# Moving work between the stages of a two-layer Mamba, attention and expert kernel: gates, decay loads, gathering, and the product delta u

## The chip, the cores and the metric

The kernel runs on one core of a Trainium2 chip. The metric is the device time in microseconds (us) of one execution; a time stated for a kernel is the median of its runs. Five engines of the core work beside each other, each on its own queue of instructions, in order: TensorE (PE) for matrix products, VectorE (DVE), ScalarE (ACT), GpSimd (POOL) and SyncE (SP). SP issues most of the loads, POOL most of the stores, and ACT some loads. Everything is float32.

## The reference

Four images of 64 x 64 tokens with 128 channels go through two layers.

```python
# layer 0: three selective scans over the 4096 tokens of an image
xz = in_proj_w @ group_norm(x)              # 256 rows for x, 256 for z
def mamba_dir(xz):                          # forward, backward, and sliced order
    x, z = split(xz)
    x = silu(causal_conv1d(x))              # called u in the kernel
    dt, B, C = split(x_proj_w @ x)          # 8, 16 and 16 rows
    delta = softplus(dt_w @ dt + dt_b)
    h = 0                                   # 256 x 16 states
    for t in tokens:
        h = h * exp(delta[t] * A) + (delta[t] * x[t]) * B[t]     # A = -exp(A_log)
        y[t] = sum_n(h * C[t])
    return (y + D * x) * silu(z)
x = x + out_proj_w @ (mamba_f + mamba_b + mamba_s)

# layer 1, attention: 16 heads of 8 channels, q = k = v
q = ring(cos(layer_norm(x) + theta))
ctx = softmax(q q^T / sqrt(8)) q            # then projection, norm, a small FFN, norm

# layer 1, experts: each of 64 experts chooses its 8 best tokens of an image
probs = softmax(gate_w @ layer_norm(t), over tokens)
topv, topi = top_k(probs, 8)
pooled[e] = sum_k topv[k, e] * layer_norm(t)[topi[k, e]]
answer[e] = [gelu([pooled[e], 1] @ weight1[e]), 1] @ weight2[e]
t[topi] += topv * answer
```

## The kernel before

The order of the work is written out by hand. Pieces of work are Python generators that yield between groups of instructions; a `Pace` hands out so many of those yields for each round of something else, and `flow(pieces, width, apart)` interleaves up to `width` pieces, the next one beginning once the one before has come `apart` yields far. The order in which instructions are handed out is the order in which each engine gets them.

**Loading.** `scan_weights` loads and transposes weights for the three scans. At its end it loads `A_log` of each direction with 32 small DMAs (0.5 KB each), half on the ACT queue and half on the POOL queue, 96 in all.

**The fill.** `Inputs.pieces` makes what the scans of all four images need. For each image it normalises x (`norm`), and then, for each of three orders and four chunks of 1024 tokens (`of_chunk`), makes u, B, C and delta and stores them in DRAM. delta is a softplus put together from ACT, PE and DVE steps (lines 400 to 427). Line 431 then multiplies delta by u, in place in the tile `u`, and stores the product `du`. `gate` computes silu(z) of one quarter of the image; its tile comes from the same pair of buffers as `u`. The four gates of an image follow the four chunks of the third order. Beside this work, `Scans.of_image(0, ...)` already scans image 0, with 1.5 yields of inputs for each yield of the scan.

**A scan.** `of_image` has 384 steps for an image: 12 chunks, each of 8 x 4 steps. A tile of 128 rows holds 16 channels with 8 states each, so two steps share a load. `load` broadcasts delta and du from DRAM (512 KB each) two steps ahead, mostly on SP. `exp` is ACT's exponential of delta A; `inputs` multiplies du by B on DVE; `step` runs the scan instruction on DVE, has POOL copy its last column into `ends`, and multiplies by C; `total` sums over states on PE, and `out` adds D u and stores. The tiles of delta have three buffers, those of du four.

**The loops.** `Attention.opening(b)` combines the scans of image b into the attention's input. `Attention.loop(b, beside)` has 1024 rounds, each with scores (`s`), softmax exponentials (`e`, two ACT instructions) and values (`acc`). Beside the loops of images 0 to 2 run the scans of the next images, and what follows or precedes an image (`after`, `opening`). These are the scanning loops. Beside the loop of image 3, called the last loop, `last` runs at 0.8 yields a round: the rest of image 2, the experts' search and choice for images 0 to 2, and image 3 block by block as far as its attention is done. `block.bank` is a single PSUM bank there.

**The tail.** After the last loop, `closing` finishes the eighth block of image 3, and `gathers` is handed out between its steps, at 3.0 yields for each. It is `experts.gather(range(nb - 1))`, 24 pieces of `pool`. Each piece loads a block of 512 normalised tokens, turns the chosen weights into columns with PE (`wt`, line 1198), copies them (`wT`, line 1204) and multiplies (`pool`, line 1209). Then come choice and gathering for image 3, the experts' weights, streamed through few rooms, and the answers scattered to the output.

Of the kernel before, what the change touches and what calls it, by code (L numbers as in the profile page):

```python
# [11 lines left out]
F32 = mybir.dt.float32  # L12
# [4 lines left out]
P = 128  # L17
# [7 lines left out]
T = 1024  # L25
# [109 lines left out]
def scan_weights(nc, const, load, load_ps, ident, in_proj_w, out_proj_w, dirs):  # L135

    w_z = const["fill"].tile([P, DI], F32, name="w_z")
    w_out = const["all"].tile([P, 2, C], F32, name="w_out")
    w_in = load.tile([P, 4, C], F32, tag="w_in", name="raw_in")
    nc.sync.dma_start(out=w_in, in_=in_proj_w.rearrange("(k p) c -> p k c", p=P))  # L140
    ps = load_ps.tile([P, 512], F32, tag="ps", name="ps_in")
    for m in range(2):
        nc.tensor.transpose(ps[:, m * P : (m + 1) * P], w_in[:, 2 + m, :], ident)
    nc.vector.tensor_copy(w_z, ps[:, :DI])
    raw = load.tile([P, DI], F32, tag="raw", name="raw_out")
    nc.sync.dma_start(out=raw, in_=out_proj_w)
    ps = load_ps.tile([P, 512], F32, tag="ps", name="ps_out")
    for m in range(2):
        nc.tensor.transpose(ps[:, m * P : (m + 1) * P], raw[:, m * P : (m + 1) * P], ident)
    nc.vector.tensor_copy(w_out.rearrange("p m c -> p (m c)"), ps[:, :DI])  # L150
    ws = []
    for i, d in enumerate(dirs):
        w = {}
        raw = load.tile([R + 2 * NS, DI], F32, tag="raw", name=f"raw_x{i}")
        nc.sync.dma_start(out=raw, in_=d["x_proj_w"])
        w["x"] = const["fill"].tile([P, 2, X_ROWS], F32, name=f"w_x{i}")
        nc.gpsimd.memset(w["x"], 0.0)
        for m in range(2):
            ps = load_ps.tile([P, 512], F32, tag="ps", name=f"ps_x{i}_{m}")
            k = R + 2 * NS  # L160
            nc.tensor.transpose(ps[:, :k], raw[:, m * P : (m + 1) * P], ident[:k, :k])
            for row, at, n in [(32 * g, 0, R) for g in range(4)] + [(B_ROW, R, NS), (C_ROW, R + NS, NS)]:
                nc.vector.tensor_copy(w["x"][:, m, row : row + n], ps[:, at : at + n])
        raw = load.tile([P, 2, X_ROWS], F32, tag="raw_dt", name=f"raw_dt{i}")
        nc.gpsimd.memset(raw, 0.0)
        for g in range(4):
            by = (nc.sync, nc.scalar)[g % 2]
            by.dma_start(out=raw[:, :, 32 * g : 32 * g + R], in_=d["dt_proj_w"].rearrange("(m p) r -> p m r", p=P))
        w["dt"] = const["fill"].tile([X_ROWS, 2, P], F32, name=f"w_dt{i}")
        ps = load_ps.tile([P, 512], F32, tag="ps", name=f"ps_dt{i}")  # L170
        for m in range(2):
            nc.tensor.transpose(ps[:X_ROWS, m * P : (m + 1) * P], raw[:, m, :], ident)
        nc.vector.tensor_copy(w["dt"].rearrange("r m p -> r (m p)"), ps[:X_ROWS, :DI])
        for name in ("conv_b", "dt_proj_b"):
            w[name] = const["fill"].tile([P, 2], F32, name=f"{name}{i}")
            nc.scalar.dma_start(out=w[name], in_=d[name].rearrange("(m p) -> p m", p=P))

        w["D"] = const["all"].tile([P, DI // 32], F32, name=f"D{i}")
        for g in range(4):
            nc.scalar.dma_start(out=w["D"][32 * g : 32 * g + 32], in_=d["D"].rearrange("(k p) -> p k", p=32))  # L180

        taps = load.tile([P, 2, 4], F32, tag="taps", name=f"taps{i}")
        nc.scalar.dma_start(out=taps, in_=d["conv_w"].rearrange("(m p) k -> p m k", p=P))
        w["conv"] = const["fill"].tile([P, 4, DI], F32, name=f"conv{i}")
        for k in range(4):
            ps = load_ps.tile([P, 512], F32, tag="ps", name=f"ps_cv{i}_{k}")
            for m in range(2):
                cut = load.tile([P, C], F32, tag="cut", name=f"cut{i}_{k}_{m}")
                nc.vector.tensor_scalar_mul(cut, w_in[:, m, :], taps[:, m, k : k + 1])
                nc.tensor.transpose(ps[:, m * P : (m + 1) * P], cut, ident)  # L190
            nc.vector.tensor_copy(w["conv"][:, k, :], ps[:, :DI])
        ws.append(w)
    for i, (d, w) in enumerate(zip(dirs, ws)):

        w["A"] = const["all"].tile([P, 2, NB // 2], F32, name=f"A{i}")
        a_log = d["A_log"].rearrange("(k d) (q n) -> d q n k", d=16, n=NS2)
        for c in range(16):
            for q, by in enumerate((nc.scalar, nc.gpsimd)):
                by.dma_start(out=w["A"][c * NS2 : (c + 1) * NS2, q, :], in_=a_log[c, q])
    return w_z, w_out, ws  # L200


class Inputs:
# [38 lines left out]
    def pieces(self, images):  # L242

        for b in images:
            self.sz[b] = self.dram.tile([DI, L], F32, name=f"d_sz_{b}")
            yield self.norm(b)
            for order in range(3):
                if order == 2:
                    yield self.slices(b)
                for c in range(NC):  # L250
                    yield self.of_chunk(b, order, c)
                    if order == 2:
                        yield self.gate(b, c)

    def norm(self, b):

# [77 lines left out]
    def of_chunk(self, b, order, c):  # L334
# [93 lines left out]
            self.leave()  # L428
        self.middle = False
        keep("delta", r)  # L430
        nc.vector.tensor_mul(u, r, u)
        keep("du", u)
        self.made[b, order, c] = made
        yield

# [1 line left out]
class Scans:  # L437
# [23 lines left out]
    def of_image(self, b, made, alone=False):  # L461
# [54 lines left out]
        def step(s):  # L516

            order, c, k, j = steps[s]
            at = 4 * k + j
            dA, dB = tiles.pop(("delta", s)), tiles["du", s]  # L520
            h = self.deep.tile([P, T], F32, tag="h", bufs=2, name=f"h_{b}_{s}")
            first = 0.0 if c == 0 else ends[order, c - 1][:, at : at + 1]
            nc.vector.tensor_tensor_scan(h, dA, dB, first, ALU.mult, ALU.add)  # L523
            if c < NC - 1:
                nc.gpsimd.tensor_copy(ends[order, c][:, at : at + 1], h[:, T - 1 :])  # L525
            if s + 1 < n:
                inputs(s + 1)
            nc.vector.tensor_mul(dB, h, spread[order, c, "C", j % 2])  # L528

        def total(s, y):  # L530
            order, c, k, j = steps[s]
# [836 lines left out]
def tile_kernel(tc, ctx, x, in_proj_w, dirs, out_proj_w, attn, gate, weight1, weight2, out):  # L1368
# [15 lines left out]
    with ExitStack() as fill:  # L1384
        consts = {"all": all_const, "fill": fill.enter_context(tc.tile_pool(name="w_fill", bufs=1))}
        with tc.tile_pool(name="w_load", bufs=2) as load, tc.tile_pool(
            name="w_load_ps", bufs=2, space=PSUM
        ) as load_ps:
            w_z, w_out, made = scan_weights(nc, consts, load, load_ps, ident, in_proj_w, out_proj_w, dirs)
        ws.extend(made)  # L1390
        inputs = Inputs(tc, fill, x, w_z, ws, cols, dram, ident)
        scans.bank = Bank(fill.enter_context(tc.tile_pool(name="s_bank", bufs=2, space=PSUM)), 2)
        with tc.manual_schedule():
            first = Pace(scans.of_image(0, inputs.made, True))
            others = Pace(flow(inputs.pieces(range(nb)), 2, 10))
            while not first.done:
                others.run(1.5)
                first.run(1.0)
            others.rest()
# [12 lines left out]
    block.bank = bank  # L1412
    loop = ExitStack()
    block.begin(loop)
    with tc.manual_schedule():
        last = Pace()
        n = 3 * NC * NB
# [32 lines left out]
    with tc.manual_schedule():  # L1450
        last = Pace(
            last.parts, experts.biases(),
            *(part for images in pairs[:-1] for part in (experts.search(images, blocks), experts.choice(images, blocks))),
            block.after(nb - 1, range(0, 4)), block.after(nb - 1, range(4, 6)), block.after(nb - 1, range(6, blocks - 1)),
            experts.search(pairs[-1], blocks - 1),
        )
        block.loop(nb - 1, lambda i: last.run(0.8), True)
        last.rest()
    loop.close()
    with ExitStack() as end:  # L1460
        block.bank = Bank(end.enter_context(tc.tile_pool(name="end_ps", bufs=7, space=PSUM)), 7)
        with tc.manual_schedule():
            room = experts.room(end, 3)
            gathers = Pace(experts.gather(range(nb - 1)))
            with ExitStack() as pieces:
                block.pieces_of(pieces, 1, opening=False)
                closing = block.after(nb - 1, range(blocks - 1, blocks), experts.rest(pairs[-1], blocks - 1))
                for i, _ in enumerate(closing):
                    if i == 2:
                        experts.prefetch(room, nc.scalar)  # L1470
                    gathers.run(3.0)
            for _ in experts.choice(pairs[-1], blocks - 1):
                gathers.run(3.0)
            gathers.rest()
            experts.prefetch(experts.room(end, 1), nc.scalar)
            for _ in experts.gather(pairs[-1]):
                pass
            for _ in experts.answers(end, out):
# [33 lines left out]
```

## Time and profile before

| What | Value |
|---|---|
| Time, median of 3 runs | 12982.96 us (12969.35 to 12983.24) |
| Profiled execution, its own time | 12992.53 us |
| Its span | 12990.6 us |
| PE busy | 12191.8 us, 94% of the span |
| ACT busy | 10713.3 us, 82% |
| DVE busy | 8718.2 us, 67% |
| POOL busy | 2930.0 us, 23% |
| DMA moved | 1481.86 MB, 114 GB/s on average |
| SP's DMA queue | 1055.63 MB, 31.8% of 16 engines' span |

The profile is of one execution. The stages follow each other: loading to about 58 us, the fill to 2273 us, the opening of image 0 to 2598, the loops of images 0 to 2 to about 10240, the last loop to 12680, then the tail. In a row of the profile, `out<-in` names the tiles, `x` the number of instructions, then come busy time in us and the mean in ns of one, and then the idle time of the engine just ahead of them with what ended it. A busy share of PE is a modelled one, and the average over the span mixes stages that different engines limit; so shares are read by stage.

### The profile page before, as it was taken

What the parts mean: (1) busy time and instruction counts of PE and PEld (TensorE: products, weight loads), DVE (VectorE), ACT (ScalarE), POOL (GpSimd) and SP (SyncE); (2) the same over time, 40 slices, a digit from 0 to 9 for tenths busy, and PEclk for the clock granted to TensorE, in tenths of its full rate; (3) what the DMA queues carried; (4) which work ended last, traced back from release to release, by engine and by line L of the source; (5) the groups of instructions that cost most, each with busy time, mean ns of one, the idle gap of its engine ahead of it and who ended that gap; (6) DMA issues with size and microseconds to landing.
All of it is one profiled execution on the core that took longest, in us unless ns stands there. A gap on an engine that the chain in (4) does not pass through costs nothing.

```text
span 12990.6 us, 213981 instructions
## 1 busy us (share of the span) xinstructions
PE 12191.8 (94%) x85447; PEld 3937.0 (30%) x85447; DVE 8718.2 (67%) x8674; ACT 10713.3 (82%) x10808; POOL 2930.0 (23%) x3817
## 2 busy tenths in 40 slices
PE   7788888399999999999999999999999999999996
PEld 3333333122222222333322223333222223322225
DVE  6999999788888777888887778888874211121112
ACT  5676766399999988999999889999998888888881
POOL 3323232221212212223232123232321000000000
PEclk9898988699999999999999999999999999999996
DMA  5666776555444455444444445444443100000005
GB/s 157 195 202 195 208 199 190 159 124 122 119 122 111 111 132 134 125 117 111 115 110 110 130 132 126 117 110 116 112 110 97 51 19 11 18 24 11 16 14 183
DMA packets 688512, 1481.86 MB, mean 114 GB/s; under 512 B 187694, under 2 KB 304998, under 8 KB 687254
## 3 DMA queue, kind: packets, MB, share of 16 engines
q1 hardware_dynamic: 499294, 1055.63, 31.8%
q0 software_dynamic: 140192, 302.80, 7.6%
q10 hardware_dynamic: 48024, 109.74, 3.3%
q8 instruction: 669, 10.96, 0.4%
q14 instruction: 333, 2.73, 0.1%
HBM read 1158.77 MB, written 308.81 MB: 113 GB/s over the span
## 4 chain that ended last, share of the span: by engine, by line
PE 81%; DVE 7%; ACT 5%; issue 4%; DMA 3%; SPq 0%; POOL 0%; ACTq 0%; DVEq 0%; POOLq 0%
PE s L881 36%; PE acc L895 30%; PE y L534 4%; PE cv L364 3%; DVE h L523 3%; PE sp L422 2%; PE fo L1033 1%; ACT e L886 1%; PE h L1023 1%; PE xd L378 1%; DVE dB L514 1%; ACT ln L415 0%; DVE du L514 0%; PE out L761 0%; DVE r L427 0%
## 5 line engine op out<-in xcount | busy, mean ns | idle before, releaser
L886 ACT ACTIVATE e<-s 128x1024 f32<-128x1024 f32 x8192 | 7904.8, 1027 | 1053.5 <-PE s L881 882.8
L881 PE MATMUL s<-qm,qT 32*128 32x512 f32 x32768 | 5444.3, 642 | 120.8 <-ACT e L886 61.5
L895 PE MATMUL acc<-e,v 128*32 128x512 f32 x32768 | 4387.5, 607 | 23.8 <-ACT av L904 21.3
L881 PEld LDWEIGHTS s<-qm,qT 32*128 32x128 f32 x32768 | 1801.7, 184 | 3239.3 <-issue 1429.4
L525 POOL COPY ends<-h 128x1 f32<-128x1 f32 x1152 | 1275.0, 1108 | 3352.1 <-DVE h L523 3322.4
L895 PEld LDWEIGHTS acc<-e,v 128*32 128x32 f32 x32768 | 649.0, 108 | 3160.9 <-issue 3021.8
L523 DVE TENSOR_TENSOR_SCAN h<-delta,ends,du 128x1024 f32<-128x1024 f32 x576 | 1350.9, 2345 | 216.2 <-ACT delta L507 185.5
L523 DVE TENSOR_TENSOR_SCAN h<-dA,ends,dB 128x1024 f32<-128x1024 f32 x576 | 1350.6, 2345 | 149.2 <-ACT dA L507 145.8
L514 DVE TENSOR_TENSOR dB<-du,B 128x1024 f32<-128x1024 f32 x768 | 927.9, 1208 | 626.8 <-PE y L534 603.6
L507 ACT ACTIVATE delta<-delta,A 128x1024 f32<-128x1024 f32 x768 | 887.0, 1155 | 153.4 <-PE y L534 142.7
L507 ACT ACTIVATE dA<-delta,A 128x1024 f32<-128x1024 f32 x768 | 888.4, 1157 | 140.9 <-DMA delta<-d_delta 105.4
L528 DVE TENSOR_TENSOR du<-h,C 128x1024 f32<-128x1024 f32 x768 | 935.3, 1218 | 0.1
L528 DVE TENSOR_TENSOR dB<-h,C 128x1024 f32<-128x1024 f32 x768 | 935.0, 1217 | 0.0
L514 DVE TENSOR_TENSOR du<-du,B 128x1024 f32<-128x1024 f32 x768 | 920.9, 1199 | 0.0
L364 PE MATMUL cv<-xn,conv 128*128 128x512 f32 x1024 | 499.9, 642 | 25.7 <-DVE xn L299 17.3
L563 POOL DMA_DIRECT2D d_y<-o x512 | 327.6, 668 | 781.9 <-DVE o L550 720.3
L910 POOL DMA_DIRECT2D d_ctx<-av x512 | 263.4, 523 | 1055.8 <-ACT av L904 1046.5
L534 PE MATMUL y<-du,sel 128*32 128x256 f32 x6144 | 488.2, 391 | 13.1 <-DVE du L528 13.1
L534 PE MATMUL y<-dB,sel 128*32 128x256 f32 x6144 | 491.7, 393 | 3.4 <-DVE dB L528 3.4
L523 DVE TENSOR_TENSOR_SCAN h<-delta,du 128x1024 f32<-128x1024 f32 x192 | 438.4, 2283 | 52.0 <-ACT delta L507 45.5
L523 DVE TENSOR_TENSOR_SCAN h<-dA,dB 128x1024 f32<-128x1024 f32 x192 | 438.4, 2283 | 40.0 <-ACT dA L507 38.4
L1026 DVE TENSOR_SCALAR h<-h,b 128x512 f32<-128x512 f32 x124 | 92.7, 748 | 514.0 <-PE s L881 514.0
(256 smaller groups left out, 7648.6 us busy)
## 6 DMA issues: line engine op xcount, KB each, us to landing
delta<-d_delta SPq DMA_DIRECT2D x768, 512.0 KB
du<-d_du SPq DMA_DIRECT2D x576, 512.0 KB
du<-d_du ACTq DMA_DIRECT2D x192, 512.0 KB
d_u<-u POOLq DMA_DIRECT2D x48, 1024.0 KB, 5.8
B<-d_bc SPq DMA_DIRECT2D x96, 512.0 KB
C<-d_bc SPq DMA_DIRECT2D x96, 512.0 KB
d_delta<-r POOLq DMA_DIRECT2D x48, 1024.0 KB, 5.1
d_du<-u POOLq DMA_DIRECT2D x48, 1024.0 KB, 6.9
```

The lines of the kernel that those rows point to most:

```text
L364: nc.tensor.matmul(ps[:, cut], w["conv"][:, k, m * P : (m + 1) * P], reads(k, g), start=(k == 0), stop=(k == 3))
L507: nc.scalar.activation(tiles["delta", s], t, AF.Exp, scale=A)
L514: nc.vector.tensor_mul(tiles["du", s], du, spread[order, c, "B", j % 2])
L523: nc.vector.tensor_tensor_scan(h, dA, dB, first, ALU.mult, ALU.add)
L525: nc.gpsimd.tensor_copy(ends[order, c][:, at : at + 1], h[:, T - 1 :])
L528: nc.vector.tensor_mul(dB, h, spread[order, c, "C", j % 2])
L534: nc.tensor.matmul(y[32 * g : 32 * g + 32, : T // 4], self.sel[:, j // 2, :], hC[:, 256 * g : 256 * g + 256], start=(j == 0), stop=(j == 3),)
L563: nc.gpsimd.dma_start(out=to.rearrange("p (i j) -> p i j", i=SLICES)[:, :, at : at + n], in_=rows.rearrange("p (i j) -> p i j", i=SLICES),)
L881: nc.tensor.matmul(s_ps[:, k, :], qT[at : at + 32, kc * P : (kc + 1) * P], queries[j, qb][at : at + 32, :], start=True, stop=True,)
L886: nc.scalar.activation(e, s_ps, AF.Exp, scale=1.0 / math.sqrt(D))
L895: nc.tensor.matmul(accs[j, qb][32 * k : 32 * k + 32, :], v[:, kc, h * VW : h * VW + 32], es[i][k // 2][:, k % 2, :], start=(kc == 0), stop ...
L910: nc.gpsimd.dma_start(out=self.context[b][h * D : h * D + D, cut], in_=av[32 * k : 32 * k + D, :])
```

## The change

Four edits, in four places.

- `scan_weights` no longer loads `A_log`. A generator `decays` does it, handed out ahead of the scan of image 0 once image 0 is normalised, with all 96 loads on SP.
- The gates of an image follow its third, sixth, ninth and twelfth chunk in place of its last four.
- Line 431 and its store remain only for chunks that `early` names: all 12 of image 0 and the first two of image 1. For the other 34 chunks, the scan makes the product. While one chunk is scanned, `product` makes the next one's, in eight parts of 128 x 256 elements: from the ninth step on, in turns of three steps, it loads a part of delta and of u on SP, lets a step pass, and then multiplies on DVE and stores on POOL. The two tiles are in a pool with one buffer for each name.
- `experts.gather` for images 0 to 2 becomes part of `last`, after each choice, and `last` runs at 0.92 yields a round. The tail no longer has `gathers`, and the last room of expert weights is filled ahead of the choice for image 3.

```diff
-    for i, (d, w) in enumerate(zip(dirs, ws)):
+    for i, w in enumerate(ws):
         w["A"] = const["all"].tile([P, 2, NB // 2], F32, name=f"A{i}")
+    return w_z, w_out, ws
+
+def early(b, order, c):
+    return b == 0 or (b == 1 and order == 0 and c < 2)
+
+def decays(nc, dirs, ws, inputs):
+    while 0 not in inputs.normed:
+        yield WAIT
+    for d, w in zip(dirs, ws):
         a_log = d["A_log"].rearrange("(k d) (q n) -> d q n k", d=16, n=NS2)
         for c in range(16):
-            for q, by in enumerate((nc.scalar, nc.gpsimd)):
-                by.dma_start(out=w["A"][c * NS2 : (c + 1) * NS2, q, :], in_=a_log[c, q])
-    return w_z, w_out, ws
+            for q in range(2):
+                nc.sync.dma_start(out=w["A"][c * NS2 : (c + 1) * NS2, q, :], in_=a_log[c, q])
+    yield
...
                     yield self.of_chunk(b, order, c)
-                    if order == 2:
-                        yield self.gate(b, c)
+                    third, at = divmod(order * NC + c, 3)
+                    if at == 2:
+                        yield self.gate(b, third)
...
-        nc.vector.tensor_mul(u, r, u)
-        keep("du", u)
+        if early(b, order, c):
+            nc.vector.tensor_mul(u, r, u)
+            keep("du", u)
...
             nc.vector.tensor_mul(dB, h, spread[order, c, "C", j % 2])
+            if not alone:
+                product(s)
+
+        def product(s):
+            order, c, k, j = steps[s]
+            part, turn = divmod(4 * k + j - 8, 3)
+            chunk = (b, order, c + 1) if c + 1 < NC else (b, order + 1, 0) if order < 2 else (b + 1, 0, 0)
+            if part < 0 or turn == 1 or chunk not in made or early(*chunk):
+                return
+            of, m, at = made[chunk], part // 4, part % 4 * (T // 4)
+            cut = slice(m * P, (m + 1) * P), slice(at, at + T // 4)
+            if turn == 0:
+                for name in ("delta", "u"):
+                    t = self.extra.tile([P, T // 4], F32, tag=f"x_{name}", name=f"x_{name}_{b}_{s}")
+                    nc.sync.dma_start(out=t, in_=of[name][cut])
+                    tiles["x", name] = t
+            else:
+                t, u = tiles.pop(("x", "delta")), tiles.pop(("x", "u"))
+                nc.vector.tensor_mul(t, t, u)
+                nc.gpsimd.dma_start(out=of["du"][cut], in_=t)
...
-            first = Pace(scans.of_image(0, inputs.made, True))
+            first = Pace(decays(nc, dirs, ws, inputs), scans.of_image(0, inputs.made, True))
...
     block.begin(loop)
+    scans.extra = loop.enter_context(tc.tile_pool(name="s_extra", bufs=1))
...
-            *(part for images in pairs[:-1] for part in (experts.search(images, blocks), experts.choice(images, blocks))),
+            *(
+                part for images in pairs[:-1]
+                for part in (experts.search(images, blocks), experts.choice(images, blocks), experts.gather(images))
+            ),
...
-        block.loop(nb - 1, lambda i: last.run(0.8), True)
+        block.loop(nb - 1, lambda i: last.run(0.92), True)
...
-            gathers = Pace(experts.gather(range(nb - 1)))
...
-                    gathers.run(3.0)
+            experts.prefetch(experts.room(end, 1), nc.scalar)
             for _ in experts.choice(pairs[-1], blocks - 1):
-                gathers.run(3.0)
-            gathers.rest()
-            experts.prefetch(experts.room(end, 1), nc.scalar)
+                pass
```

## The prediction

> **What bounds the kernel now.** I read it by stage, since one average over the span hides four different limits. First the 40 slices of the page, then the table of stages (busy time of each engine, granted clock, DMA share), then the waits inside each stage, last the chain of waits at both ends.
>
> ```profile
> PE   7788888399999999999999999999999999999996
> DVE  6999999788888777888887778888874211121112
> ACT  5676766399999988999999889999998888888881
> ```
>
> ```profile
> 130.00:2273.00 2143.00, 1799.08 (x6639) 718.52 (x6639) 2017.62 (x1453) 1493.42 (x1196) 696.79 (x841) 0.88 0.68 199
> 2598.00:10240.00 7642.00, 7554.91 (x58997) 2245.27 (x58991) 5978.63 (x5585) 7035.06 (x7322) 1925.67 (x2461) 0.99 0.47 116
> 10240.00:12680.00 2440.00, 2417.21 (x17254) 709.12 (x17248) 368.36 (x947) 2017.03 (x2110) 178.81 (x313) 0.99 0.07 20
> 12680.00:12860.00 180.00, 138.15 (x572) 120.83 (x573) 51.25 (x133) 10.73 (x17) 15.13 (x27) 0.53 0.37 124
> ```
>
> The columns after the length are PE, PEld, DVE, ACT, POOL, clock, DMA share, GB/s. The fill (130 to 2273 us) is DVE's: 2018 of 2143 us, 94%, while ACT stands at 70% and PE at 84%. DVE's named waits there come to some 100 us, none over 7.2 us. The three loops that carry scans (2598 to 10240) and the last loop belong to PE at 99%; there DVE is at 78%, then 15%. ACT is close behind PE in the scanning loops (92%), so they have little room for an ACT stall. The tail runs PE at half clock.
>
> ```profile
> L431 DVE TENSOR_TENSOR u<-r,u 128x2048 f32<-128x2048 f32 x48 | 110.0, 2292 | 1.7
> L514 DVE TENSOR_TENSOR dB<-du,B 128x1024 f32<-128x1024 f32 x768 | 927.9, 1208 | 626.8 <-PE y L534 603.6 <-DMA du<-d_du 22.8
> L1209 PE MATMUL pool<-wT,x 128*128 128x64 f32 x256 | 60.9, 418 | 40.9 <-DVE wT L1204 27.0 <-DMA x<-d_xn 13.9
> L1198 PE MATMUL wt<-diagonal,chosen 64*128 64x64 f32 x256 | 60.4, 411 | 0.7 <-ACT av L904 0.7
> ```
>
> L431 is the product delta u, all 48 in the fill. L514's 604 us behind PE's y is DVE slack, nearly all in the loops. L1209 and L1198 are the gathering, all in the tail.
>
> ```profile
> 12749.59 1.90 PE wt L1198 x8
> ...
> 12761.74 1.03 PE wt L1198 x8
> ```
>
> ```profile
> 12640.54 1.30 PE s L881 x8
> 12641.84 0.99 PE acc L895 x8
> 12642.84 1.07 PE s L881 x8
> 12643.91 0.99 PE acc L895 x8
> ```
>
> In the chain, eight gathering matmuls take 1.90 us at half clock and 1.03 at full. An undisturbed pair of attention rounds takes 4.36 us, 2.18 a round; 1024 rounds would be 2232 us, and the last loop takes 2440.
>
> ```profile
> 47.09 1.28 ACT L274 ACT_TABLE_LOAD   x1 [47.09 <-DMA A<-in_L_conv_A_log_s_dram]
> ```
>
> At the start ACT, issuing decay loads, comes to its first copy at 48.4 us, although the transposes for it begin at 33.7.
>
> **What the Trainium skill says.** "Perfetto Trace Analysis", section "Optimization Strategy", says that a kernel can have regimes with different most-contended engines and that interleaving them may pay: the stage table agrees. "TensorE: Matmul & The Clock Gate", section "What's actually happening", gives two clock states, half after an idle window; 1.90 against 1.03 us agrees. Prices: "VectorE: DVE Perf Modes", section "The TRN2 errata", gives (N+151)/0.96 ns for an f32 tensor_tensor; N = 2048 gives 2291 ns against 2292 here. "DMA: Bandwidth & Descriptors", section "Anatomy of one DMA", gives 2.0 us + bytes/436e3; the 256 KB stores of d_xn land in 2.4 us here, 2.6 by the formula.
>
> **Part 1, the start.** 48 loads leave the ACT queue and 48 the POOL queue; SP gets 96. ACT can copy at about 36 us. The third and fourth x groups land at 40.5 us and about 42.5 (the first fetch took 4.9 us from issue), so the statistics that end at 54.3 us end near 46 to 47: **-8 us**. On SP the 96 issues follow the x loads from 38 us. At 0.4 to 0.6 us each (ACT's rows: 7.0 us for 16, POOL's 9.4 for 16) they end by 76 to 96 us. Queued behind them are the first scan loads, which wait until 119 us for delta now and would until 111: covered. If each takes ACT's worst 0.92 us (14.76 for 16), they end at 126 and the gain becomes a loss of 6. Bounds -12 and +6.
>
> **Part 2, the fill.** L431 stays for 14 early chunks (12 of image 0, 2 of image 1) and goes for 34: 34 x 2.292 = 78 us of DVE, with 34 POOL stores of 0.72 us and 34 MB of writes. DVE is the bound and its 6% idle shrinks with it: 78/0.94 = 83. The tile u is also freed after the x projection. The gates are the same work (16 x 8 matmul instructions, 5.3 us of ACT table loads and 2.0 us of Silu each), only no longer bunched in the last third: counting the order in which pieces are handed out, both streams still end together. Bunched table loads cost DVE some stalls (4.9 us at 2144); I credit none. What could come next is the softplus chain of PE and ACT waits (PE sp behind ACT 160 us), so I take **-80 us**; bounds -40 (half) and -100.
>
> **Part 3, the products in the scanning loops.** 34 chunks x 8 pieces = 272 multiplications of 128x256; (256+151)/0.96 = 424 ns, so 115 us of DVE in 7642, on an engine with 604 us of slack behind PE. 544 loads and 272 stores of 128 KB add 107 MB to some 890: DMA share 0.47 to 0.53. POOL gets 272 x 0.6 = 163 us on 25% busy. SP gets 544 issues of about 0.5 us.
> The new wait: each buffer exists once, so a piece's delta load waits on SP for the store of the piece before (0.6 issue + 2.3 landing, about 3 us after its multiplication). Behind it on SP stand the next delta and du broadcasts; ACT's decay exponential waits for those, and the softmax exponentials behind that. In a stretch at 3300 us, the broadcast so delayed would be issued some 10 us before its exponential, and a broadcast lands in about 5 to 6 us: covered. The multiplication follows its loads by two scan steps of 5 to 6 us. I take **+5 us**; bounds 0 and +60.
>
> **Part 4, gathering beside the last loop.** 24 of 32 pieces move, each with a group of eight wt and eight pool instructions: 48 x 1.03 = 49 us of PE. The loop absorbs nothing: from 10492 to 11396 us, 754 exponentials are 377 rounds, 822 us by themselves; the other 82 us are PE work of eight blocks, 10 us each, about what its matmuls take at full clock. Twice wt may wait for chosen (two passes of 4.4 us on DVE), some 2.5 us each: **+54 us**; bounds +30 and +65. SP's x loads and DVE's copies (0.42 + 0.26 us a piece) are hidden by DMA share 0.07 and an idle DVE.
> Hand-out order: at 0.8 a round, counting yields puts search of the first pair at round 492, the trace at 11408 us, about 490. At 0.92, gathering ends at round 658, and the work on the last image's seventh block ends some ten yields after the loop. Those leave a transpose, a gate matmul, a store, a reload and a 4.4 us maximum in front of the closing reciprocal: +5.
>
> **Part 5, the tail.** The closing chain loses the gathering groups it now queues behind: 4.5 us at the second co, 6 at zt, 13 between the h matmuls, 7.5 between fo, 6.6 around xT and lg, 37.5 together. After choice, four old pieces at 4.4 us no longer stand before the last image's eight, less a fresh start of 5: 12.5. So -50, with the spill **-45 us**; bounds -30 and -60. The last weight room is filled before choice, but the 23 MB stream of the other weights (60 us at 386 GB/s) stays whole and starts sooner with the first answer.
>
> **Sum**: -8 - 80 + 5 + 54 - 45 = -74. The profiled execution took 12992.5 (span 12990.6), 9.6 above the median 12983; the same difference off the median gives **12909 us**. Nearly all of it is the fill: gathering about pays for itself.
>
> **The rivals.**
> *Slower: SP's new wait starves ACT.* Every second piece sits directly before a broadcast needed two steps later: 136 events. If each stalls ACT and PE by 1.1 us net, +150 replaces +5: 71 slower, **13054**. It decides above 0.54 us an event, and needs landings beyond 10 us. For it: ACT at 92%, SP in order. Against: 18 us of such waits now, and SP already waits 4597 us on PE's y without harm. 8%.
> *The fill is half bound elsewhere.* PE and ACT chains of the softplus take over once DVE is relieved: -40 for -80: **12949**. For: the 160 us of PE waits and a granted clock of 0.88. Against: DVE at 94%. 17%.
> *Gathering is cheaper than 1:1, and unbunched gates give more*: last loop +30, tail -55, fill -95: -123 with the rest, **12860**. For: every second s takes 1.30 rather than 1.07. Against: the 1:1 count. 18%.
> *It doesn't do what it says*: gathering delays the last image's blocks and more spills behind the loop; 60 yields instead of ten, about 50 us: **12959**. Against: the count. 5%.
> *Forecast*: 52%.
>
> **How the numbers follow.** About 0.2%, 26 us, is what this kernel's measurement can tell from no change. Faster: forecast, cheap gathering, most of the half-bound fill and half of the spill, less a tenth for mixtures: 0.84. Same 0.07, slower 0.09. The range takes in 12860 with some margin and both milder rivals: 12835 to 12965.
>
> **What would show it.** Right: the fill's end near 2185 instead of 2273; L431 14 times; a 128x256 product 272 times at about 0.42 us; first copy near 36 us; scanning loops within 15 us of 7642; last loop near 2495; from its end to the last output about 265 instead of 310. Wrong: ACT decay exponentials waiting for delta by over 100 us in the loops, DVE below 90% in the fill, or the seventh block's work long after the last round.

## The result, and the profile after

The changed kernel takes 12908.8 us (median of 5 runs, 12900.7 to 12916.6) against 12983.0 us before; the ratio is 0.9948, with a 95% interval from 0.9933 to 0.9962. The profiled execution took 12908.77 us, with a span of 12907.1. The forecast was 12909. The total agrees, its terms do not. That they add up to the measured value is luck: the fill gave 18 us less than forecast, the last loop and the tail together 30 us more.

To see that, the span is cut at marks that every kernel has: the first convolution matmul, the load of `cos_ry` on the ACT queue (it ends the fill), the first score, the first load of `sum` in the last loop, and the last score. Each mark is the start of an instruction in the trace.

| Stage (us) | before | after | difference | forecast |
|---|---|---|---|---|
| start, to the first convolution | 59.1 | 49.5 | -9.6 | -8 |
| fill, to the load of `cos_ry` | 2195.4 | 2133.8 | -61.6 | -80 |
| opening of image 0, to the first score | 256.5 | 253.6 | -2.9 | 0 |
| scanning loops | 7737.8 | 7749.0 | +11.2 | +5 |
| last loop | 2427.4 | 2465.3 | +37.9 | +54 |
| tail, from the last score | 314.4 | 255.9 | -58.5 | -45 |
| span | 12990.6 | 12907.1 | -83.5 | -74 |

The profiled execution of before was 9.6 us above its median and that of after is at its own, so 83.5 us of span are 74 us of median; the forecast's 74 was a sum over the span, and measured by the span it is 9.5 us short. How far a stage of one execution can be read shows in the kernels below that leave it alone: fill 2189 to 2195, scanning loops 7738 to 7740, last loop 2421 to 2427, tail 310 to 317. Differences under some 6 us say little.

First the 40 slices of the page of the changed kernel, then its stages (length, busy us and number of instructions of PE, PEld, DVE, ACT and POOL, granted clock, DMA share, GB/s).

```profile
PE   7888887599999999999999999999999999999996
DVE  7999998788888877888887778888874211101112
ACT  5676766499999988999999889999998888888882
```

```profile
120.00:2183.00 2063.00, 1766.58 (x6596) 708.93 (x6596) 1923.28 (x1399) 1497.50 (x1197) 727.38 (x795) 0.90 0.66 189
2524.00:10180.00 7656.00, 7560.65 (x58991) 2240.79 (x58992) 6065.96 (x5857) 7036.30 (x7324) 2117.20 (x2734) 0.99 0.51 130
10186.00:12651.00 2465.00, 2446.62 (x17556) 745.82 (x17556) 371.59 (x964) 2007.03 (x2100) 171.65 (x302) 1.00 0.07 20
12651.00:12720.00 69.00, 24.70 (x87) 12.91 (x80) 32.05 (x91) 6.88 (x9) 13.54 (x24) 0.57 0.48 159
```

The slices look nearly the same. The stages show the move: the closing block in the tail now has PE idle for most of 69 us, where gathering used to fill it, and the last loop is still full. DVE stands at 93% of the fill (1923 of 2063), as it did before. By this alone one would say again that DVE bounds it; the experiments show what that is worth.

The instructions of the product came out as costed. From the line's own view, line 446 (431 before) and the product in the loops:

```profile
L446 DVE TENSOR_TENSOR u<-r,u x14: 2291/2292/2293, 104.5 to 700.7; 128x2048 f32<-128x2048 f32 x14
```

```profile
L563 DVE TENSOR_TENSOR x_delta<-x_delta,x_u x272: 406/420/433, 2617.9 to 9562.2; 128x256 f32<-128x256 f32 x136
```

From the page, the first tile product of a scan step (with its slack behind PE's y, 604 us before) and the new stores:

```profile
L529 DVE TENSOR_TENSOR dB<-du,B 128x1024 f32<-128x1024 f32 x768 | 929.6, 1210 | 657.1 <-PE y L570 595.0
...
L564 POOL DMA_DIRECT2D d_du<-x_delta x272 | 154.4, 568 | 1132.2 <-DVE x_delta L563 1069.1
```

From the groups of the last loop, gathering, three quarters of it (192 of 256 matmuls of each kind):

```profile
L1245 PE MATMUL pool<-wT,x 128*128 128x64 f32 x192 | 26.5, 281 | 0.0
L1234 PE MATMUL wt<-diagonal,chosen 64*128 64x64 f32 x192 | 26.4, 278 | 0.0
```

And from the timeline of ACT, its first copy, at 48.4 us before:

```profile
34.50 1.01 ACT L288 COPY xn<-xt 128x1024 f32<-128x1024 f32 x1 [0.71 <-PE xt L286]
```

### The profile page after: what moved, and what is told of

Same layout as the page of the kernel before. It is cut to its first block, busy times and chain, and to the rows that moved or that the text cites. A ratio compares the mean times of both kernels' runs of the same rounds, so it can differ in the third digit from the quotient of the medians.

```text
span 12907.1 us, 215600 instructions
## 1 busy us (share of the span) xinstructions
PE 12125.7 (94%) x85447; PEld 3883.9 (30%) x85447; DVE 8730.9 (68%) x8912; ACT 10718.9 (83%) x10812; POOL 3129.4 (24%) x4007
## 4 chain that ended last, share of the span: by engine, by line
PE 80%; DVE 7%; ACT 5%; issue 4%; DMA 3%; SPq 1%; POOL 0%; ACTq 0%; DVEq 0%; POOLq 0%
PE s L917 36%; PE acc L931 29%; PE y L570 4%; PE cv L378 3%; DVE h L538 3%; PE sp L436 2%; PE fo L1069 1%; ACT e L922 1%; PE h L1059 1%; PE xd L392 1%; DVE dB L529 1%; DMA du<-d_du 1%; DMA w<-in_L_ffn_weight_dram 0%; DMA d_y<-o 0%; ACT e L424 0%
## 5 line engine op out<-in xcount | busy, mean ns | idle before, releaser
L540 POOL COPY ends<-h 128x1 f32<-128x1 f32 x1152 | 1375.3, 1196 | 2875.1 <-DVE h L538 2866.0
L564 POOL DMA_DIRECT2D d_du<-x_delta x272 | 154.4, 568 | 1132.2 <-DVE x_delta L563 1069.1
```

## The experiments

### Each part of the change alone

The change was split into its four parts, each applied alone to the kernel before. Their diffs are the four parts of the diff above; the product's part has `early`, `product`, `s_extra` and the condition around line 431.

> The kernel before with the products of the 34 late chunks moved into the scanning loops, and nothing else (gates bunched, decay loads on ACT and POOL, gathering in the tail). Theory 1, the fill's gain is this part's alone and is all that a DVE-bound fill gives: fill 61 us shorter (the whole change's fill), loops 11 us longer, median 45 to 55 below before. Rival, the spread gates cost the fill DVE waits (behind PE's y they grew by 21 us in the whole change): without them the fill shrinks by about 80 us, median 65 to 70 below before. Rival, the gates brought part of it: fill shrinks by 40 us or less, median 30 below or less.

> The kernel before with the gates spread over an image's chunks, and nothing else. Theory 1: the same work in the same engines under a DVE that is the bound, fill unchanged within 5 us, median within 10 of before. Rival, the spread gates cost waits on PE: fill 20 us longer. Rival, unbunched table loads and Silus free DVE: fill 20 us or more shorter.

> The kernel before with gathering for images 0 to 2 beside the last loop at 0.92 yields a round and the last weight room filled ahead of the last choice, and nothing else. Theory 1, the parts add up: last loop 38 us longer and tail 58 us shorter as in the whole change, 20 below before, fill and scanning loops unchanged within 3 us. Rival, the tail's gain in the whole change came partly from elsewhere: tail only 45 us shorter, median within 10 of before.

> The kernel before with the 96 decay loads on SP, and nothing else. Theory 1: the first convolution matmul comes 9 to 10 us sooner and all that follows keeps this, median 8 to 12 below before. Rival, the fill gives it back, since the first scan loads stand behind 96 issues on SP: first convolution sooner, fill longer by as much, median within 4 of before.

| Part alone | median us | to before (12984.0) | ratio, 95% interval | stage that moved (before: fill 2195, last loop 2427, tail 314) |
|---|---|---|---|---|
| product | 12970.7 | -13.3 | 0.9982 to 0.9999 | fill 2169.9, loops 7754.7 |
| gates | 12958.4 | -25.5 | 0.9975 to 0.9988 | fill 2168.6 |
| gathering | 12960.8 | -23.1 | 0.9975 to 0.9990 | last loop 2459.3, tail 253.4 |
| decay loads | 12968.5 | -15.5 | 0.9985 to 0.9998 | start 49.6 (from 59.1) |

The four add up to -77 us; the whole change gave -74. Gathering and the decay loads do alone what they do in the whole. So both their rivals fall: the tail lost 61 us with gathering alone and not 45, and the fill does not give the start back, being 2189.2 us with the decay loads alone. The median of the decay loads alone fell by 15.5 us, beyond the 8 to 12 that were expected, but its interval, some 3 to 19, takes these in. But the fill's gain is not the product's. Moving 78 us of DVE work out made the fill 26 us shorter (22 against 2191.5, the mean of the three kernels that leave the fill alone) and the loops 17 longer. Spreading the gates, credited with nothing in the forecast, made it 27 (23) shorter. Both theories for the product alone, 61 and 80 us, are refuted, and so is "unchanged" for the gates; the rivals that gave the gates a share are right. Together the two parts give 59 to 62, some 9 to 15 us more than the two alone add up to.

The busy time of each engine over the fill, in the kernel before, with the product alone and with the gates alone (the line of the changed kernel, 120 to 2183 us, stands above):

```profile
120.00:2254.00 2134.00, 1795.83 (x6611) 717.43 (x6610) 2001.30 (x1437) 1497.48 (x1200) 691.46 (x833) 0.89 0.69 200
```

```profile
120.00:2229.00 2109.00, 1791.38 (x6612) 713.71 (x6610) 1928.55 (x1404) 1497.14 (x1200) 688.90 (x800) 0.89 0.65 186
```

```profile
120.00:2228.00 2108.00, 1775.10 (x6608) 710.79 (x6606) 1997.70 (x1435) 1503.93 (x1204) 673.47 (x829) 0.90 0.69 202
```

The third number after the length is DVE. The product alone takes 73 us off its busy time, and its idle time rises from 133 to 180: two thirds of what was freed turned into waiting. The gates alone leave the busy time as it was and take the idle time from 133 to 110. They save no work on ACT either: its busy time (the fourth number) is 1504 us with them and 1497 before, so fewer table loads are not the reason.

Where the idle time sits with bunched gates is seen in two neighbouring stretches of image 2's inputs: 1250 to 1500 us, which has no gate in the kernel before, and 1500 to 1700, which has all four. First the kernel before, then the one with spread gates.

```profile
1250.00:1500.00 250.00, 218.97 (x818) 88.13 (x808) 248.32 (x175) 183.05 (x145) 82.22 (x103) 0.91 0.69 201
...
1500.00:1700.00 200.00, 166.47 (x619) 64.58 (x617) 181.77 (x128) 143.74 (x117) 60.77 (x90) 0.91 0.70 205
```

```profile
1250.00:1500.00 250.00, 211.48 (x797) 83.97 (x796) 247.39 (x174) 188.18 (x149) 72.76 (x103) 0.92 0.70 209
1500.00:1700.00 200.00, 159.79 (x642) 66.11 (x640) 192.31 (x145) 136.61 (x111) 71.78 (x92) 0.88 0.75 220
```

Before, DVE idles 1.7 us in the first stretch and 18.2 in the second; with spread gates 2.6 and 7.7. The two longest waits of DVE between 1500 and 1700 us in the kernel before (what waited, for whom, us, times, longest) say for whom:

```profile
DVE h L523 <- ACT delta L507: 9.1, 3, 5.0
DVE h L523 <- ACT dA L507: 4.2, 4, 3.5
```

DVE waits for the scan's exponentials on ACT; with spread gates these two waits are 4.1 us together in the same stretch. A gate brings work for PE and ACT and none for DVE, so bunched gates let DVE fall idle in one third of an image and leave it full in the other two.

This doesn't explain the price of the product. If a saving on DVE were lost in one third of an image only, two thirds of the 78 us would be paid out, 52; measured are 22 to 26. With the gates spread it is more, 35 us (from 2168.6 in the kernel with the gates alone to 2133.8), but still less than half.

### Bunched, but elsewhere

```diff
-                    if order == 2:
+                    if order == 0:
                         yield self.gate(b, c)
```

> The kernel before with the four gates of an image bunched behind the chunks of its first order in place of its third. Theory (gates carry no DVE work, so bunched they leave DVE waiting for ACT's exponentials in one third of an image, while it is full in the other two): no gain, fill 2185 to 2200 us from the first convolution to the load of cos_ry, as in the kernel before (2195) and in the two kernels that leave the fill alone (2189, 2190). Rival, it is their place at an image's end that costs: fill at 2175 us or less, as with spread gates (2169).

The median is 13015.0 us, ratio 1.0023 (1.0014 to 1.0031). The fill takes 2207.6 us, the opening 268.2 (256.5 before). So it is not the place at an image's end that costs. That it became 12 to 18 us longer was expected by neither theory, nor was the opening's 12 us; both stay open. The same two stretches, in this kernel, show what bunching does. Here three of image 2's four gates lie between 1250 and 1500 us (the first is at 1220) and none between 1500 and 1700:

```profile
1250.00:1500.00 250.00, 224.97 (x796) 87.52 (x797) 230.88 (x162) 189.58 (x154) 72.44 (x101) 0.91 0.67 199
1500.00:1700.00 200.00, 170.29 (x628) 68.74 (x627) 196.30 (x140) 145.62 (x115) 66.71 (x89) 0.86 0.71 211
```

DVE now idles 19.1 us in the first stretch, where it was 1.7, and 3.7 in the second, where it was 18.2, and 16.9 of the 19.1 are again waits of the scan for ACT's exponentials. The idle time went where the gates went. So the bunch causes it; what moving the bunch cost besides isn't explained by this run.

### What a microsecond of each engine is worth in the fill

```diff
-        if early(b, order, c):
-            nc.vector.tensor_mul(u, r, u)
-            keep("du", u)
+        nc.vector.tensor_mul(u, r, u)
+        if early(b, order, c):
+            keep("du", u)
```

> The changed kernel, in which the 34 late chunks of the fill run line 446's multiplication again (34 x 2.29 = 78 us of DVE), without storing its result, which nobody reads. Theory (the fill is bound in part by DVE and in part by the order in which PE and ACT serve its chains, so that a microsecond of DVE is worth about half of one): fill 30 to 45 us longer. Rival, DVE is the bound at 1:1: fill 75 to 85 us longer. Rival, DVE's time is not what the fill gained by, the stores and the tile u were: fill within 10 us of the changed kernel.

```diff
-        nc.scalar.activation(s, e, AF.Identity, bias=1.0)
-        nc.scalar.activation(s, s, AF.Identity, bias=self.minus_one)
...
-    ((self.ident, e), (self.minus, s), (self.ident, ln))
+    ((self.ident, e), (self.minus, e), (self.ident, ln))
```

> The changed kernel, in which the softplus of the fill leaves out the two ACT instructions that make s (48 x (1.92 + 2.00) = 188 us of ACT) and PE subtracts e in its place; the rounding correction is left out so. Theory (ACT's and PE's chains hold part of the fill): fill 30 to 100 us shorter. Rival, DVE is the bound alone: fill within 10 us of the changed kernel.

```diff
-                for i, (sign, t) in enumerate(((self.ident, e), (self.minus, s), (self.ident, ln))):
-                    nc.tensor.matmul(ps[:, cut], sign, t[:, m, cut], start=(i == 0), stop=(i == 2))
+                nc.tensor.matmul(ps[:, cut], self.ident, ln[:, m, cut], start=True, stop=True)
```

> The changed kernel, in which the softplus sums one term on PE in place of three (768 fewer matmuls of 0.59 us, 454 us of PE at most, about 227 us where the records overlap); the correction of the logarithm's rounding is left out. Theory: part of the fill's DVE and ACT waits end on PE, fill 20 to 80 us shorter. Rival, DVE is the bound alone: fill within 10 us of the changed kernel.

The fill's busy times again, DVE's multiplications back, ACT lightened, PE lightened:

```profile
120.00:2215.00 2095.00, 1770.83 (x6596) 709.51 (x6596) 1995.80 (x1431) 1497.94 (x1197) 664.74 (x795) 0.90 0.65 186
```

```profile
120.00:2114.00 1994.00, 1728.86 (x6593) 701.89 (x6591) 1915.71 (x1394) 1317.86 (x1100) 722.21 (x795) 0.92 0.68 195
```

```profile
120.00:2136.00 2016.00, 1509.06 (x5851) 588.61 (x5850) 1921.33 (x1399) 1497.38 (x1195) 735.26 (x796) 0.85 0.67 193
```

| Against the changed kernel | engine's busy time | fill | fill per us of the engine |
|---|---|---|---|
| DVE's multiplications back (median 12942.0) | DVE +72.5 | +30.7 | 0.42 |
| ACT without s (median 12837.9) | ACT -179.6 | -69.1 | 0.38 |
| PE with one term (median 12869.1) | PE -257.5 | -48.8 | 0.19 |

All three are within what the theory named, though its ranges were wide, and the rival, DVE as the only bound, is refuted on each count. A microsecond of DVE is worth 0.4, though DVE is busy 93% of the time, and one of ACT, busy 73%, is worth nearly as much. The Trainium skill ("Perfetto Trace Analysis", section "Identifying the Most-Contended Engine") tells one to find the engine with the highest occupancy, its share of busy time, and to optimize that first; for DVE and ACT it also calls occupancy a fair measure of how near the engine is to its peak. Here that finds DVE, but not what a microsecond of it is worth: for this the measurement decides. In the first of these kernels the multiplication runs 48 times again and stores nothing more, so the 31 us are not the stores'. It also holds the tile `u` for longer, as before; that part isn't separated from DVE's time. The second and third, which compute less, are measurements of ACT and PE and no candidates.

### The product's new wait on SP

```diff
-    t = self.extra.tile([P, T // 4], F32, tag=f"x_{name}", ...)
+    t = self.extra.tile([P, T // 4], F32, tag=f"x_{name}", bufs=2 if name == "delta" else 1, ...)
```

> The changed kernel with two buffers in place of one for the product's delta tile, so that SP's load no longer waits for the store of the piece before. Theory, this wait is hidden: scanning loops within 5 us of the changed kernel's 7749 us (first sum load to last), although SP's wait of 2102 us on d_du goes. Rival, it is what made the loops 11 us longer: 8 us or more come back.

The waits of SP in the loops, in the changed kernel and with two buffers:

```profile
SPq L508 <- PE y L570: 2841.8, 346, 24.8
SPq L559 <- DMA d_du<-x_delta: 2101.9, 236, 23.6
```

```profile
SPq L508 <- PE y L570: 3431.6, 429, 24.8
SPq L559 <- DVE x_delta L563: 1223.3, 225, 20.5
```

The wait for the store is gone, and the loops take 7743.6 us instead of 7749.0. By this pair that is 5 us, at the edge of what a stage can be read to; the median is 12903.6 (ratio to before 0.9939, 0.9920 to 0.9959). The other kernels say more. The seven that make the product in the loops with one buffer take 7749.0 to 7758.1 us there, 7753 in the mean, the two with two buffers 7743.6 and 7744.7, and the five without the product 7737.5 to 7740.1. By these means the product costs the loops about 15 us and the wait some 9 of them. So the rival is nearer than the theory: the wait is not hidden, though its 2102 us on SP's queue cost only some 9. By which way they reach PE and ACT is open. In the changed kernel the wait mostly takes the place of the wait on PE's y (4597 us before), and ACT's exponentials wait 19.1 us for delta in the loops, 18.5 before.

### Gathering issued twice

```diff
-        for i in range(4):
+        for i in [0, 1, 2, 3] * (2 if b + 1 < self.nb else 1):
```

(in both loops of `pool`)

> The changed kernel in which the gathering of images 0 to 2, beside the last loop, issues each of its wt and pool matmuls twice (48 more groups of eight). Theory, a group's records overlap its neighbours', so a group costs less than its 1.03 to 1.10 us of record: last loop 33 to 42 us longer. Rival, 1:1 by the records: 49 to 53 us longer. Rival, PE had room: under 15 us.

The groups of the last loop:

```profile
L1245 PE MATMUL pool<-wT,x 128*128 128x64 f32 x384 | 48.0, 278 | 0.0
L1234 PE MATMUL wt<-diagonal,chosen 64*128 64x64 f32 x384 | 47.9, 275 | 0.0
```

48 more groups of eight made the last loop 38.8 us longer (2504.1), 0.81 us each, and the median 12956.7. This is the theory's value, and PE had no room for them. But their records are shorter than assumed: 95.9 us for all groups here against 52.9 in the changed kernel, 0.90 for each one added, so that this run alone hardly tells 38.8 from one to one. The first 48 groups tell it: they cost 32 us alone and 38 in the whole change, 0.67 to 0.79 each, where their records are 1.10. The records of the loop's groups of matmuls add up to 2668 us in the changed kernel (all rows of that view), and PE's busy time to 2447: they overlap their neighbours'. The same section of the skill calls the busy share of matmuls no good measure of how near PE is to its peak, because pipelined PE instructions look smaller in the trace. Here it is no good price either, and the records are larger than what the groups cost.

### The leftover behind the loop

```diff
-        block.loop(nb - 1, lambda i: last.run(0.92), True)
+        block.loop(nb - 1, lambda i: last.run(1.0), True)
```

> The changed kernel with the last loop's other work at 1.0 yields a round in place of 0.92, so that nothing of image 3's seventh block is left behind the loop. Theory, what was left behind helped by accident: its buffers held the weight rooms back until 20 us after the last score, so the 6 MB of weights didn't fill the DMA queues while the closing block's sums went through DRAM; without it the time from the last score to the last match-replace (80 us in the changed kernel) grows by 3 to 12 us, or stays. Rival, as forecast, the leftover costs 5 us there: it shrinks by 4 us or more. Last loop 0 to 4 us longer in both.

The median is 12908.6, no different. From the last score to the last match-replace it takes 77.3 us (12657.0 to 12734.3), against 80.3 in the changed kernel (12651.2 to 12731.5). The seven kernels with the leftover and the same prefetch take 79.4 to 81.5 us for it, so 77.3 lies outside their range. The leftover did not help; the theory that it kept the queues free by accident falls. Its rival's sign is right, with 3 us in place of 4 or more.

### The weights off ACT's queue

```diff
-                for i, _ in enumerate(closing):
-                    if i == 2:
-                        experts.prefetch(room, nc.scalar)
-            experts.prefetch(experts.room(end, 1), nc.scalar)
+                for _ in closing:
+                    pass
+                experts.prefetch(room, nc.sync)
+            experts.prefetch(experts.room(end, 1), nc.sync)
```

> The changed kernel with two buffers for the product's delta tile, and with the prefetch of all four weight rooms on SP's queue behind the closing block in place of ACT's queue in its middle. Theory: ACT's closing sine comes 2 us sooner and its exponentials of the last choice 3.5 us sooner, the weights still land before the first answer needs them; tail 5 to 8 us shorter, loops 0 to 6 us shorter, median 12896 to 12904. Rival, the weights now come too late for the first answers: tail longer than the changed kernel's 256 us.

In the chain of the changed kernel, ACT's sine waits behind weight DMAs that ACT itself issues, and its exponentials of the last choice wait for the fourth room's:

```profile
12672.51 9.65 DMA w<-in_L_ffn_weight_dram
...
12683.04 6.97 DMA w<-in_L_ffn_weight_dram
12690.00 1.28 ACT L1118
...
12724.20 1.09 ACTq L1265
12725.32 1.28 ACT L1204
```

With the prefetch on SP both are gone from the chain, and what is late next is the leftover block's logits, which go through DRAM to a maximum on DVE ahead of the closing normalisation:

```profile
12663.06 3.51 DMA d_lg<-lgs
12666.63 7.39 DMA prob<-d_lg
12674.04 3.89 DVE best L1184
```

The tail takes 248.6 us, 7.3 less (4 to 7 less than in the other kernels with gathering moved and the rate 0.92, 253.0 to 255.9), the loops 7744.7, 4.3 less, and the median is 12899.6 (ratio 0.9933, 0.9918 to 0.9948), 9 below the changed kernel's. The stages moved as the theory said, the loops by the second buffer, and the weights came in time. The intervals of the two kernels overlap, so by the medians alone the gain isn't separated; of the kernels that leave nothing out, this is the fastest that was run. The last chain suggests a rate of 1.0 on top of it; that was not tried.

## Why the prediction was right, and where not

The total, 12909, is what was measured, but by errors that cancel. The forecast promised 25 us too much in the fill and the loops together, and 34 us too little in the start, the opening, the last loop and the tail. The 9.5 us left over are hidden by the 9.6 us by which the profiled execution of before ran above its median. The steps, one by one:

**Part 1, the start (-8).** Right: -9.6. The copy comes at 34.5 us. The 96 issues on SP run from 36.2 to 76.2 us, 0.42 each from one to the next, as in the early end of the estimate.

**Part 2, the fill (-80).** The step that failed is "78/0.94 = 83", and with it "I credit none" for the gates. DVE's busy share was read as a price of one to one. Measured, the product's removal gives 22 to 26 us with bunched gates and 31 to 35 with spread ones, the gates 23 to 27, and both together some 60. So the first term was more than twice too large and the second was taken as nothing; that these errors partly cancel is why -80 is only 18 off. The rival "half bound elsewhere" had the mechanism and was still too high with 40; the rival "unbunched gates give more" had the other half. The sign that I had named for a wrong forecast, DVE below 90% in the fill, did not appear: DVE lost 78 us of work and the fill 62 us of time, so its share stayed at 93%. The sign could not tell the two theories apart. The hint was in the trace of before: in image 2's inputs the stretch with gates has DVE at 91% and the one ahead of it at 99%, and a stage average of 94% hid it.

**Part 3, the loops (+5).** Within its bounds, but too low: +11 in the whole change, +17 for the part alone, some 15 by all kernels. That the multiplications hide in DVE's slack is right, though most of it was not where I looked: over the loops, line 529's wait behind PE's y fell by 30 us (580 to 551), the scan's waits for ACT's exponentials by 65 (356 to 291), and the wait of the output step, o, behind y by 22. What failed is "covered" for the new wait on SP, which cost some 9 us. The DMA share rose from 0.47 to 0.51, not 0.53. The rival of a starved ACT is refuted: the expected wait of over 100 us on delta stayed at 19.

**Part 4, the last loop (+54).** The mechanism, no room on PE, is right; the size of a group was off. I priced it at its record in the chain, 1.03 us; it costs 0.7 to 0.8. The two waits for `chosen` that I added at 2.5 us each do not show among PE's waits in the loop.

**Part 5, the tail (-45).** Right in kind, -58.5. From the last score to the last match-replace it is -43.0, where I had -37.5 for gathering groups and +5 for the leftover. Without a leftover (the kernel at 1.0) it is -46, so the groups were worth 46 and not 37.5. The difference lies from zt to lg, 59.4 us before and 27.5 in that kernel, 31.9 less where 27 were counted: the count missed the three groups between zt and the first h (12725.83 to 12732.11 in the chain before). Some 3 us more went between lg and the match-replace. From there to the first answer it is -15.6 against -12.5, as the fresh start of the gathering cost less than the 5 us allowed. The rest, 130.6 us before and 130.7 after, is unchanged, as forecast.

So "gathering about pays for itself" is wrong too: alone it gives 23 us, nearly a third of the whole, and the product, which the change is mostly made of, gives 13.

## What to carry to other kernels

A busy share of 94% is not a price: before taking work off an engine, cut its stage into stretches and look where it idles and for whom, and test the price by adding or removing known work. Here, in a stage where DVE, ACT and PE wait for one another, a microsecond of the busiest one was worth 0.3 to 0.45. Work that leaves the busiest engine out is worth spreading through the stage; here this gave as much as taking 78 us off that engine. For matmuls that go between others, price a group by the time that the stage grows, not by its records, and try to keep DMA issues off the queue of an engine that a closing chain needs.

## What the runs showed that was not expected

- In the fill, ACT at 73% busy was worth 0.38 us for each of its microseconds, nearly the 0.42 of DVE at 93%. The three values for DVE, ACT and PE (0.42, 0.38, 0.19) add up to about 1, as if the fill were one chain that passes through all three; this reading of them was not tested.
- Issuing DMAs can hold up ACT itself: four issues of a weight room took 2.34 us on ACT's queue at 12673.0 us, and the next four 7.66; its sine stood behind them. Why the later ones took longer no view shows.
- The queue of SP issued the decay loads no faster than ACT's did at its best: 32 in 13.4 us, 0.42 each, against 16 in 7.0 us on ACT (0.44) and 16 in 9.4 on POOL (0.59). So the start did not gain by faster issues. ACT's first copy had stood behind 16 that took 14.8 us, while what stands behind them on SP was not late: the fill did not lengthen with the decay loads alone.
